# A graph layer's weighted one-hots: two wide VectorE operations per six chunks, or six tensor_scalar operations with place and weight as scalars

## The chip, the cores and the metric

The kernel runs on one core of a Trainium2 chip. The metric is the time on the device in microseconds (us), the median of three runs. A profile of one further execution was taken; all durations below come from it.

## The reference, cut to what matters

```python
# first layer: a weighted sum over edges (200,000 edges sorted by dst, 12,500 nodes of 256 numbers)
msgs = layernorm(x)[src] * edge_weight[:, None]
agg  = segment_sum(msgs, dst)            # indices sorted
x    = x + agg @ W.T + b
# second layer: a graph attention over 131,072 other edges gives each node four gates;
# four experts (256 -> 512 -> 256, gelu) run on every node
y    = layernorm(x)
x    = x + sum_e gate[:, e] * (gelu(y @ W1[e] + b1[e]) @ W2[e] + b2[e])
```

Everything is float32. The change concerns the first layer's `agg`.

## The kernel before, in words

The kernel has four stages, one after another. First, the inputs are normalised and written to DRAM as rows (`z_rows`), and the edge lists are turned into tiles. Second comes the gather stage, which is where the change lies. Third, `agg` goes through W, is normalised again and is stored. Fourth, the four experts run, beside the attention's gathers and scans, and after them the gates and the output.

In the gather stage the 200,000 edges are cut into chunks of 128 edges, one edge in each partition. Six chunks (`GQ = 6`) are a group, and there are 261 groups (`NQ`). The destinations are sorted, so all edges of a group usually lie within a window of 128 nodes that begins at the group's first destination. The function `window` (L485) makes the window's sum:

- For each chunk, GpSimd (POOL) issues one indirect DMA that fetches the 128 source rows of `z_rows` into a third of a tile `gt` (L497). The pool of `gt` has six such tiles, two to a group, so POOL can be up to three groups ahead of the readers.
- VectorE (DVE) makes six weighted one-hot matrices of 128 x 128, as one tile `oh_w`. The entry in row p and column l is the edge's weight where the destination's place in the window (mod 128, `lo_q`) is l, and else zero. The pool of `oh_w` has two such tiles.
- TensorE (PE) multiplies the six one-hots with the six row blocks and sums them in a PSUM tile `win` (L509). A float32 product is two matmul records and two weight loads.
- `add_window` (L511) adds `win` to the accumulator `acc_x` in two operations, one for each of the two node tiles that a window can touch (L515).

Before the change the one-hots take two VectorE operations. `spread_hot` (L312) compares a table of column numbers, each number twice, with the six places: a tensor_tensor in bfloat16 into `hit_w` (L316). A second tensor_tensor multiplies it with the weights into `oh_w`, float32, and reorders it on the way (L503):

```python
hit = spread_hot(hot, lo[:, s], P, "hit_w", GQ, 1)
oh = hot.tile([P, GQ, P], F32, name="oh_w")
nc.vector.tensor_mul(oh.rearrange("p (k i) l -> p k i l", i=2), hit.rearrange("p k l i -> p k i l"), ...)
```

Beside the groups runs a counting sort of the second layer's edges. In the first 32 groups (`early`) PE counts places (`count`, L330). At group 32 `sort_begin` (L359) turns the counts into starting places through small tables (`cn`, `inc`, `node`, `has`, `last`, `begin`). In the other 229 groups the generator `sort_all` emits its 1035 steps evenly, 4.5 to a group. A step is a chain on PE and ScalarE (ACT): a look-up (`look`, L411 and L413), an addition of one-hots (`place`, L416), a copy by ACT (`next`, L419) and a move (`perm`, L450) whose moving operand `st` DVE makes with one tensor_scalar (L444). For each eight steps DVE also makes the one-hots `oh_hi`, `oh_lo` and `to_p` (L316), two selections `sel` (L424) and `pos` (L426), and four small operations on eight numbers (L435 to L438).

Each engine runs its own list in order. The lists are made by a planner that goes by its own estimates of duration; a change in an operation can therefore change the order in which the planner puts others beside it. An instruction that waits holds up all that are behind it on its engine.

A further branch, which repeats `window` for groups that reach beyond one window, is guarded by a value computed at run time; in the profile L497 ran for 1563 chunks and L503 for 261 groups, which is once per group.

Of the kernel before, what the change touches and what calls it, by code (L numbers as in the profile page):

```python
# [23 lines left out]
F32 = mybir.dt.float32  # L24
# [3 lines left out]
BF = mybir.dt.bfloat16  # L28
AF = mybir.ActivationFunctionType
ALU = mybir.AluOpType  # L30
# [4 lines left out]
P = 128  # L35
N, D = 12500, 256
NT = 98
# [3 lines left out]
GQ = 6  # L41
NQ = (E + GQ * P - 1) // (GQ * P)
TB = 8
# [17 lines left out]
def gnn_gat_moe(ctx, tc, x, src, dst, edge_weight, W, b, W_gat, att_src, att_dst, b_gat, ln_gamma,  # L61
                ln_beta, W1, b1, W2, b2, edge_index, out):
    nc = tc.nc
# [65 lines left out]
    free = first_two.tile([P, P], F32, name="free")  # L129
# [33 lines left out]
    with ExitStack() as s1:  # L163
        edges = s1.enter_context(tc.tile_pool(name="edges", bufs=1))
# [58 lines left out]
        for g in range(NG):  # L223
            t0, n, _ = rows_of(g)
# [21 lines left out]
        as_int = prep.tile([P, NQ * GQ], I32, name="chunk_rows_f")  # L246
        nc.vector.tensor_copy(as_int, dst_f)
        nc.vector.tensor_scalar(as_int, as_int, P - 1, None, ALU.bitwise_and)
        lo_q = edges.tile([P, NQ * GQ], BF, name="lo_q")
        nc.vector.tensor_copy(lo_q, as_int)  # L250
        beyond = prep.tile([P, NQ * GQ], F32, name="chunk_rows_f")
        nc.vector.tensor_scalar(beyond, ahead.rearrange("p q j -> p (q j)"), float(P), float(P),
# [18 lines left out]
        for k in range(0, NQ, P):  # L271
            n = min(P, NQ - k)
# [36 lines left out]
        hot = s1.enter_context(tc.tile_pool(name="hot", bufs=2))  # L309
        gat = s1.enter_context(tc.tile_pool(name="gathered", bufs=6))  # L310

        def spread_hot(pool, v, width, name, n=TB, bufs=2):  # L312

            t = pool.tile([P, n // 2, width, 2], BF, name=name, bufs=bufs)
            shape = [P, n // 2, width, 2]
            nc.vector.tensor_tensor(  # L316
                t, twice[:, None, :width, :].to_broadcast(shape),
                v.rearrange("p (k i) -> p k i", i=2)[:, :, None, :].to_broadcast(shape),
                ALU.is_equal)
            return t  # L320
# [8 lines left out]
        count2 = acc.tile([NT, P], F32, name="place")  # L329
# [4 lines left out]
                nc.tensor.matmul(into, one(oh, i), one(ol, i), start=(c0 + i == 0),  # L334
                                 stop=(c0 + i == total - 1))

        def prefix(counts, name):

            cn = edges.tile([NT, P], F32, name="cn_" + name)
            nc.vector.tensor_copy(cn, counts)  # L340
            rs = small.tile([NT, 1], F32, name="row_sum")
            nc.vector.tensor_reduce(rs, cn, AX.X, ALU.add)
            pp = bank()
            nc.tensor.matmul(pp[:NT, 0, 0:1], after[:NT, :NT], rs, start=True, stop=True)
            first = small.tile([NT, 1], F32, name="first")
            nc.vector.tensor_copy(first, pp[:NT, 0, 0:1])
            inc = edges.tile([NT, P], F32, name="inc_" + name)
            nc.vector.tensor_tensor_scan(inc, ones[:NT, :], cn, first, ALU.mult, ALU.add)
            return cn, inc

# [6 lines left out]
        state = {}  # L357

        def sort_begin():  # L359
            cn, inc = prefix(count2, "2")  # L360
            node = edges.tile([NT, P], F32, name="node")
            nc.gpsimd.iota(node, pattern=[[1, P]], base=E2, channel_multiplier=P,
                           allow_small_or_imprecise_dtypes=True)
            has = edges.tile([NT, P], F32, name="has")
            nc.vector.tensor_scalar(has, cn, 0.0, None, ALU.is_gt)
            by_node(has, has2)
            last = edges.tile([NT, P], F32, name="last")
            nc.vector.tensor_scalar(last, inc, -1.0, 0.0, ALU.add, ALU.max)
            by_node(last, end2)
            begin = edges.tile([NT, P], F32, name="begin")  # L370
            nc.vector.tensor_sub(begin, inc, cn)
            nc.vector.tensor_sub(last, begin, node)
            nc.vector.tensor_mul(last, last, has)
            nc.vector.tensor_add(last, last, node)
            by_node(last, seg2)

            place = state["place"] = acc.tile([NT, P], F32, name="place")
            nc.tensor.matmul(place, ident[:NT, :NT], begin, start=True, stop=False,
                             skip_group_check=True)
            state["next"] = begin  # L380
# [109 lines left out]
        def window(q, idx, lo, w, chunks):  # L490

            n = len(chunks)
            rows = [gat.tile([P, GQ // 2, D], F32, name="gt") for _ in range(2)]
            rows = [rows[j * 2 // GQ][:, j % (GQ // 2), :] for j in range(n)]
            for j in range(n):
                c = chunks[0] + j
                nc.gpsimd.indirect_dma_start(out=rows[j], out_offset=None, in_=Z,  # L497
                                             in_offset=IND(ap=idx[:, c:c + 1], axis=0))

            s = slice(chunks[0], chunks[0] + GQ)  # L500
            hit = spread_hot(hot, lo[:, s], P, "hit_w", GQ, 1)
            oh = hot.tile([P, GQ, P], F32, name="oh_w")
            nc.vector.tensor_mul(oh.rearrange("p (k i) l -> p k i l", i=2),  # L503
                                 hit.rearrange("p k l i -> p k i l"),
                                 w[:, s].rearrange("p (k i) -> p k i", i=2)[:, :, :, None]
                                 .to_broadcast([P, GQ // 2, 2, P]))
            win = ps.tile([P, D], F32, name="win")
            for j in range(n):
                nc.tensor.matmul(win, oh[:, j, :], rows[j], start=(j == 0), stop=(j == n - 1))  # L509
            return win  # L510

        def add_window(at, win, m0, m1):
# [6 lines left out]
        for q in range(NQ):  # L519
            if q % 4 == 0:  # L520
                n = min(4, NQ - q)
# [4 lines left out]
            win = window(q, src1, lo_q, w1,  # L526
                         [c for c in range(c0, c0 + GQ) if c * P < E])
# [19 lines left out]
        with tc.If(further > 0):  # L547
            shift = edges.tile([P, 1], F32, name="shift")
            idx4 = edges.tile([P, GQ], I32, name="idx4")
            lo4 = edges.tile([P, GQ], F32, name="lo4")  # L550
            lob4 = edges.tile([P, GQ], BF, name="lob4")
            node4 = edges.tile([P, GQ], I32, name="node4")
            w4 = edges.tile([P, GQ], F32, name="w4")
            ahead4 = edges.tile([P, GQ], F32, name="ahead4")
            below4 = edges.tile([P, GQ], F32, name="below4")
            m01 = edges.tile([P, 2], F32, name="m01")
            with tc.For_i(0, NQ, 1) as q:
                nc.vector.memset(shift, 0.0)
                n = nc.values_load(more[0:1, bass.ds(q, 1)], min_val=0, max_val=NT,
                                   skip_runtime_bounds_check_because=BOUND)  # L560
                with tc.For_i(0, n, 1) as j:
                    nc.vector.tensor_scalar_add(shift, shift, float(P))
                    nc.vector.tensor_copy(idx4, src1[:, bass.ds(q * GQ, GQ)])
                    nc.vector.tensor_copy(w4, w1[:, bass.ds(q * GQ, GQ)])
                    nc.vector.tensor_copy(ahead4, further_by.rearrange("p q j -> p (q j)")[
                        :, bass.ds(q * GQ, GQ)])
                    nc.vector.tensor_copy(m01[:, 0:1], first_f[:, bass.ds(q, 1)])
                    nc.vector.tensor_scalar(lo4, ahead4, m01[:, 0:1], None, ALU.add)
                    nc.vector.tensor_copy(node4, lo4)
                    nc.vector.tensor_scalar(node4, node4, P - 1, None, ALU.bitwise_and)  # L570
                    nc.vector.tensor_copy(lob4, node4)
# [6 lines left out]
                    win = window(q, idx4, lob4, w4, range(GQ))  # L578
# [110 lines left out]
    with ExitStack() as s3:  # L689
# [71 lines left out]
        t = pre.tile([P, L2], F32, name="scan")  # L761
# [49 lines left out]
        with ExitStack() as s5:  # L811
# [22 lines left out]
            for g in range(NG):  # L834
                t0, n, _ = rows_of(g)
# [3 lines left out]
                for e in range(C):  # L839
# [60 lines left out]
        v = by_head(end, f[:, 1, :])  # L900
# [160 lines left out]
```

## Time and profile before

| what | value |
|---|---|
| median of three runs | 5190.45 us (5141.08, 5190.45, 5194.08) |
| the profiled execution's own time | 4425.88 us |
| its span, first to last instruction | 4424.1 us |
| granted TensorE clock, mean over the span | 0.909 |
| gather stage, first gather to last window added | 154.8 to 2290.6 us |
| POOL gathers L497 | 1563, mean 1059 ns |
| VectorE L316 into `hit_w` | 261, median 550 ns |
| VectorE L503 into `oh_w` | 261, mean 948 ns |
| TensorE L509 | 3126 records, mean 402 ns |

The profile gives the busy time of each engine, the idle time ahead of each group of instructions with what ended it, and the instructions in order of time. The median of the runs is 764.6 us above the profiled execution. The views describe the profiled execution only.

### The profile page before, as it was taken

The page shows a single profiled execution, that of the slowest core. Times are in us where ns is not written, and L with a number is a line of the kernel's source. Part 1 is how long each engine was busy: PE and PEld are TensorE (multiplying, and loading weights), DVE is VectorE, ACT ScalarE, POOL GpSimd, SP SyncE. Part 2 cuts the span into 40 slices and gives each one's busy share as a digit, 9 for nine tenths or more (in the row PEclk, how much of TensorE's full clock was granted, in tenths as well). Part 3 has the DMA queues.
Part 4 walks back from the last instruction along what each step waited for, and adds up shares of the span by engine and source line. Part 5 has one row for each costly group of instructions (what it writes and reads, how often), then busy time and mean ns, then how long its engine had stood idle before and what let it go on. Part 6 is the DMA issues. An engine that isn't in the chain of part 4 may idle for free. (4 is left out here: it accounts for less than half of the span.)

```text
span 4424.1 us, 54111 instructions
## 1 busy us (share of the span) xinstructions
PE 3583.0 (81%) x19146; PEld 2567.4 (58%) x19347; DVE 2584.5 (58%) x6116; ACT 1000.2 (23%) x2139; POOL 2956.1 (67%) x2822
## 2 busy tenths in 40 slices
PE   1377999999999999999988849899999989999000
PEld 0265766766676666667667736566656656566000
DVE  5577888888888888888875441221221221221368
ACT  5100322322222222222322112121221221222000
POOL 0477777777777777777765467777777777770720
PEclk6788999999999999999998769999999999999555
DMA  6433333333333333333335552222222222221759
GB/s 216 131 92 94 97 97 97 100 97 98 98 98 98 97 98 97 99 98 98 97 106 152 136 130 56 60 65 56 69 66 56 67 54 65 65 62 44 224 121 375
DMA packets 330548, 456.42 MB, mean 103 GB/s; under 512 B 82471, under 2 KB 258753, under 8 KB 328993
## 3 DMA queue, kind: packets, MB, share of 16 engines
q0 software_dynamic: 114128, 217.01, 20.1%
q1 hardware_dynamic: 163279, 204.96, 13.9%
q10 hardware_dynamic: 52866, 30.96, 2.3%
q8 instruction: 152, 2.49, 0.2%
q14 instruction: 123, 1.01, 0.1%
HBM read 332.00 MB, written 120.72 MB: 102 GB/s over the span
## 5 line engine op out<-in xcount | busy, mean ns | idle before, releaser
L497 POOL DMA_INDIRECT gt<-z_rows,src x1563 | 1655.4, 1059 | 628.1 <-issue 351.4
L712 POOL DMA_INDIRECT G<-gat_nodes,order x1024 | 1033.0, 1009 | 341.3 <-issue 291.7
L509 PE MATMUL win<-gt,oh_w 128*128 128x256 f32 x3126 | 854.2, 402 | 208.8 <-DMA gt<-z_rows,src 117.1
L509 PEld LDWEIGHTS win<-gt,oh_w 128*128 128x128 f32 x3126 | 560.9, 195 | 380.9 <-DMA gt<-z_rows,src 219.5
L852 PE MATMUL po<-w,hh 128*128 128x256 f32 x3136 | 708.6, 384 | 71.5 <-DVE fo L854 63.2
L854 DVE TENSOR_TENSOR fo<-po,b 128x256 f32<-128x256 f32 x392 | 165.6, 424 | 1018.5 <-PE po L852 1003.0
L852 PEld LDWEIGHTS po<-w,hh 128*128 128x128 f32 x3136 | 603.1, 193 | 200.2 <-DVE fo L854 66.0
L844 PE MATMUL ph<-yt,w 128*128 128x512 f32 (+1 forms) x1600 | 696.0, 588 | 3.1 <-DMA w<-in_L_ffn_W 3.1
L419 ACT ACTIVATE next<-place 98x128 f32<-98x128 f32 x1023 | 282.4, 276 | 1396.3 <-PE place L416 1395.1
L444 DVE TENSOR_SCALAR st<-along,place_l,code 128x1024 bf16<-128x1024 f16 x1024 | 548.8, 566 | 33.8 <-PE perm L450 23.2
L450 PE MATMUL perm<-st,to_p 128*128 128x512 bf16 x1848 | 549.3, 381 | 4.5 <-DVE st L444 2.8
L844 PEld LDWEIGHTS ph<-yt,w 128*128 128x128 f32 x1600 | 307.2, 192 | 335.3 <-issue 322.7
L846 ACT ACTIVATE hh<-ph,b 128x512 f32<-128x512 f32 (+1 forms) x400 | 270.3, 678 | 988.0 <-PE ph L844 979.9
L413 PE MATMUL look<-next,oht 98*128 98x128 f32 x2046 | 471.1, 312 | 0.8 <-ACT next L419 0.7
L413 PEld LDWEIGHTS look<-next,oht 98*128 98x128 f32 x2046 | 309.6, 190 | 172.7 <-ACT next L419 129.9
L515 DVE SCALAR_TENSOR_TENSOR acc_x<-win,in,acc_x 128x256 f32 x522 | 249.7, 478 | 253.2 <-PE win L509 252.4
L503 DVE TENSOR_TENSOR oh_w<-hit_w,w 128x768 f32<-128x768 bf16 x261 | 247.6, 948 | 0.5
L416 PE MATMUL place<-oh_lo,oh_hi 128*98 128x128 bf16 x1023 | 229.1, 224 | 0.4 <-ACT next L419 0.4
L411 PE MATMUL look<-oh_lo,same_hi 128*128 128x128 bf16 x1024 | 220.3, 220 | 5.7
L450 PEld LDWEIGHTS <-to_p 128*128 128x128 bf16 x2048 | 173.3, 98 | 55.8 <-issue 5.8
L424 DVE TENSOR_TENSOR sel<-look,oh_lo 128x512 f32<-128x512 f32 x256 | 175.3, 685 | 25.0 <-PE look L413 23.7
L402 ACT ACTIVATE same_hi<-bank 128x512 bf16<-128x512 f32 x256 | 152.9, 597 | 141.7 <-PE bank L401 135.6
(274 smaller groups left out, 3628.9 us busy)
## 6 DMA issues: line engine op xcount, KB each, us to landing
expert_rows<-fo SPq DMA_DIRECT2D x96, 512.0 KB, 2.8
fo_in<-expert_rows SPq DMA_DIRECT2D x24, 2048.0 KB, 14.9
gt<-z_rows,src POOLq DMA_INDIRECT x1563
xt<-in_x SPq DMA_DIRECT2D x48, 512.0 KB, 5.1
G<-gat_nodes,order POOLq DMA_INDIRECT x1024
z_rows<-xt ACTq DMA_DIRECT2D x24, 512.0 KB, 3.0
x_rows<-x SPq DMA_DIRECT2D x24, 512.0 KB, 5.6
y_t<-yt SPq DMA_DIRECT2D x48, 256.0 KB, 6.0
```

The lines of the kernel that those rows point to most:

```text
L413: nc.tensor.matmul(look[:, i % GT, :], b["oht"][:, i, :], state["next"], start=False, stop=True)
L419: nc.scalar.activation(nxt, place, AF.Copy)
L444: nc.vector.tensor_scalar(st, along, b["l"][:, i:i + 1], code2[:, c:c + 1], ALU.is_equal, ALU.mult)
L450: nc.tensor.matmul(perm[:, h, :], to_p, st[:, h * 512:(h + 1) * 512], start=(c == 0), stop=(c == NC2 - 1), skip_group_check=True)
L497: nc.gpsimd.indirect_dma_start(out=rows[j], out_offset=None, in_=Z, in_offset=IND(ap=idx[:, c:c + 1], axis=0))
L503: nc.vector.tensor_mul(oh.rearrange("p (k i) l -> p k i l", i=2), hit.rearrange("p k l i -> p k i l"), w[:, s].rearrange("p (k i) -> p k i ...
L509: nc.tensor.matmul(win, oh[:, j, :], rows[j], start=(j == 0), stop=(j == n - 1))
L515: nc.vector.scalar_tensor_tensor(to, win, m, to, ALU.mult, ALU.add)
L712: i = nc.gpsimd.indirect_dma_start(out=G[:, t + 1, :HC + H], out_offset=None, in_=NODE, in_offset=IND(ap=order[:, t:t + 1], axis=0))
L844: nc.tensor.matmul(ph[:, :n * P], w_1[:, e, k, f * P:(f + 1) * P], yt[:, k, :n * P], start=(k == 0), stop=(k == 1))
L846: nc.scalar.activation(hh[:, f, :n * P], ph[:, :n * P], AF.Gelu, bias=b_1[:, e * NF + f:e * NF + f + 1])
L852: nc.tensor.matmul(po, hh[:, f, i * P:(i + 1) * P], w_2[:, e, f, :], start=(f == 0), stop=(f == NF - 1))
```

## The change

Each chunk's one-hot becomes one tensor_scalar: the float32 row of column numbers (`free`) is compared with the chunk's place as one per-partition scalar and multiplied by the chunk's weight as a second one. Six of these write the six parts of `oh_w`. The tile `hit_w` is gone, and the places `lo_q` are kept in float32 rather than bfloat16. The first matmul of a group gets an explicit dependency on the last of the six operations. The small tables of `sort_begin` no longer have tiles of their own: they lie in one tile taken from the pool of `gt`, so that the iota that fills `node` moves on POOL from the start of the kernel to between two gathers of group 32. In the guarded branch the bfloat16 copy `lob4` of the places goes away likewise.

```diff
-        lo_q = edges.tile([P, NQ * GQ], BF, name="lo_q")
+        lo_q = edges.tile([P, NQ * GQ], F32, name="lo_q")
...
-        def prefix(counts, name):
-            cn = edges.tile([NT, P], F32, name="cn_" + name)
+        def prefix(counts, table):
+            cn = table[:, 0, :]
...
-            inc = edges.tile([NT, P], F32, name="inc_" + name)
+            inc = table[:, 1, :]
...
         def sort_begin():
-            cn, inc = prefix(count2, "2")
-            node = edges.tile([NT, P], F32, name="node")
+            table = gat.tile([P, GQ // 2, D], F32, name="gt").rearrange("p a (b e) -> p (a b) e", e=P)
+            table = table[:NT]
+            cn, inc = prefix(count2, table)
+            node, has, last = (table[:, k, :] for k in (2, 3, 4))
...
-            s = slice(chunks[0], chunks[0] + GQ)
-            hit = spread_hot(hot, lo[:, s], P, "hit_w", GQ, 1)
             oh = hot.tile([P, GQ, P], F32, name="oh_w")
-            nc.vector.tensor_mul(oh.rearrange("p (k i) l -> p k i l", i=2),
-                                 hit.rearrange("p k l i -> p k i l"),
-                                 w[:, s].rearrange("p (k i) -> p k i", i=2)[:, :, :, None]
-                                 .to_broadcast([P, GQ // 2, 2, P]))
+            for j in range(n):
+                c = chunks[0] + j
+                last = nc.vector.tensor_scalar(oh[:, j, :], free, lo[:, c:c + 1], w[:, c:c + 1],
+                                               ALU.is_equal, ALU.mult)
             win = ps.tile([P, D], F32, name="win")
             for j in range(n):
-                nc.tensor.matmul(win, oh[:, j, :], rows[j], start=(j == 0), stop=(j == n - 1))
+                i = nc.tensor.matmul(win, oh[:, j, :], rows[j], start=(j == 0), stop=(j == n - 1))
+                if j == 0:
+                    tc.add_manual_dep(i.ins, last.ins.name, mybir.DependencyInfo(
+                        mybir.DependencyClass.Sync, mybir.DependencyReason.DATA),
+                        reason="all the one-hots of the group")
             return win
```

More of the change, by code (lines that the diff above doesn't have):

```diff
@@ L310, in gnn_gat_moe, with spread_hot @@
         gat = s1.enter_context(tc.tile_pool(name="gathered", bufs=6))
-        def spread_hot(pool, v, width, name, n=TB, bufs=2):
-            t = pool.tile([P, n // 2, width, 2], BF, name=name, bufs=bufs)
-            shape = [P, n // 2, width, 2]
+        def spread_hot(pool, v, width, name):
+            t = pool.tile([P, TB // 2, width, 2], BF, name=name)
+            shape = [P, TB // 2, width, 2]
             nc.vector.tensor_tensor(
@@ L359, in sort_begin @@
         def sort_begin():
-            cn, inc = prefix(count2, "2")
-            node = edges.tile([NT, P], F32, name="node")
+            table = gat.tile([P, GQ // 2, D], F32, name="gt").rearrange("p a (b e) -> p (a b) e", e=P)
+            table = table[:NT]
+            cn, inc = prefix(count2, table)
+            node, has, last = (table[:, k, :] for k in (2, 3, 4))
             nc.gpsimd.iota(node, pattern=[[1, P]], base=E2, channel_multiplier=P,
                            allow_small_or_imprecise_dtypes=True)
-            has = edges.tile([NT, P], F32, name="has")
             nc.vector.tensor_scalar(has, cn, 0.0, None, ALU.is_gt)
             by_node(has, has2)
-            last = edges.tile([NT, P], F32, name="last")
             nc.vector.tensor_scalar(last, inc, -1.0, 0.0, ALU.add, ALU.max)
@@ L550, in gnn_gat_moe @@
             lo4 = edges.tile([P, GQ], F32, name="lo4")
-            lob4 = edges.tile([P, GQ], BF, name="lob4")
             node4 = edges.tile([P, GQ], I32, name="node4")
@@ L570, in gnn_gat_moe @@
                     nc.vector.tensor_scalar(node4, node4, P - 1, None, ALU.bitwise_and)
-                    nc.vector.tensor_copy(lob4, node4)
+                    nc.vector.tensor_copy(lo4, node4)
                     nc.vector.tensor_scalar(ahead4, ahead4, shift, None, ALU.subtract)
@@ L577, in gnn_gat_moe @@
                     nc.vector.tensor_copy(m01[:, 1:2], in1[:, bass.ds(q, 1)])
-                    win = window(q, idx4, lob4, w4, range(GQ))
+                    win = window(q, idx4, lo4, w4, range(GQ))
                     a = nc.values_load(tile0[0:1, bass.ds(q, 1)], engines=(mybir.EngineType.DVE,),
```

## The prediction

> **What bounds the kernel now.** I read the page's groups of instructions first, then the stretches of the gather stage, then GpSimd's waits in it, then the instructions in order of time. Three engines look full in the gather stage, so busy shares don't decide it:
>
> ```profile
> L497 POOL DMA_INDIRECT gt<-z_rows,src x1563 | 1655.4, 1059 | 628.1 <-issue 351.4
> L509 PE MATMUL win<-gt,oh_w 128*128 128x256 f32 x3126 | 854.2, 402 | 208.8 <-DMA gt<-z_rows,src 117.1
> L503 DVE TENSOR_TENSOR oh_w<-hit_w,w 128x768 f32<-128x768 bf16 x261 | 247.6, 948 | 0.5
> ```
>
> In a steady stretch (columns: stretch, length, then PE, weight loads, DVE, ACT, POOL):
>
> ```profile
> 1000.00:1500.00 500.00, 472.31 (x3183) 345.66 (x3239) 432.81 (x908) 146.60 (x382) 387.53 (x370) 1.00 0.34 98
> ```
>
> 370 gathers are 61.7 groups, so a group takes 8.11 us. PE has 0.45 us of it idle, DVE 1.09, POOL 1.82. But PE's idle time ends with a gather's landing (L509 above), and POOL's waits in the sort part of the stage, last column the longest, say what its idle time is:
>
> ```profile
> POOL gt L497 <- issue: 301.1, 988, 0.3
> POOL gt L497 <- PE win L509: 29.6, 97, 0.3
> ```
>
> No wait exceeds 0.3 us, whatever is named: it is a fixed gap of 0.305 us behind every gather, not a wait for a buffer. 1562 gaps are 476 us, and with 152 us before the first gather that is all of the 628 idle. So POOL issues without a stop from 154.8 us to 2286.3: 1563 x (1.059 + 0.305) = 2132 us, the whole stage. PE works off a group 2.5 to 4.2 us after its last gather, and a window is added about 13 us before its buffer is wanted again: the others follow POOL.
>
> What can POOL save? The tile's own view has least, median and longest:
>
> ```profile
> L497 POOL DMA_INDIRECT gt<-z_rows,src x1563: 942/949/2273, 154.8 to 2285.3; - x196
> ```
>
> A gather takes 0.945 us unless something stretches it; 1563 x (1.059 - 0.945) = 178 us are stretch. The timeline shows by what:
>
> ```profile
> 1201.78 0.94 DVE L503 TENSOR_TENSOR oh_w<-hit_w,w 128x768 f32<-128x768 bf16 x1
> 1201.91 1.62 POOL L497 DMA_INDIRECT gt<-z_rows,src  x1 [0.30 <-PE bank L401]
> ...
> 1203.84 0.95 POOL L497 DMA_INDIRECT gt<-z_rows,src  x1 [0.30 <-issue]
> ...
> 1204.72 0.95 DVE L503 TENSOR_TENSOR oh_w<-hit_w,w 128x768 f32<-128x768 bf16 x1
> ...
> 1205.10 1.39 POOL L497 DMA_INDIRECT gt<-z_rows,src  x1 [0.31 <-issue]
> ...
> 1216.36 1.71 DVE L444 TENSOR_SCALAR st<-along,place_l,code 128x1024 bf16<-128x1024 f16 x3
> ...
> 1217.16 1.04 POOL L497 DMA_INDIRECT gt<-z_rows,src  x1 [0.30 <-issue]
> ```
>
> The gather at 1201.91 is 0.68 too long: what ran 0.12 us after its start, `oh_w`, ended 0.81 after it. At 1205.10 it is 0.44, with the end at 0.57. So a gather reads something 0.12 us in and waits until the wide operation ends. The gather among three `st`, 1.71 us without a break, loses only 0.09.
>
> [...] `st`, if it starts 0.16 us or more before the gather's read, delays it, and if later is itself delayed, so that the lock begins some 0.27 us into its 0.54. [...]
>
> **The change part by part.**
>
> *Removed: stretch.* I assigned every stretched gather to the two-input tensor_tensor running 0.12 us after its start. `oh_w`: 158 gathers, 67 us; `hit_w`: 51 gathers, 16 us, together 83. Check: an operation holding a lock for L delays a gather by L*L/(2 x 1.364) on average. The lock seems to begin 0.15 us in, so L is 0.80 and 0.40 us: 0.235 + 0.059 us per group, 77 us for 261. Value -83, ends -70 and -95. `oh_hi`, `oh_lo`, `to_p` (48 us) and `st` with the unassigned (43) stay; more gathers meet them per us, but there is less time: nothing.
>
> *Added: the locks of 1563 tensor_scalars of 128x128.* The nearest row is L105, float32, two per-partition scalars, 256 columns:
>
> ```profile
> 2340.60 1.36 DVE L105 TENSOR_SCALAR y<-x,mv,rstd 128x256 f32<-128x256 f32 x4
> ```
>
> One takes 0.406 us (its median); start to start it is (1.36 - 0.406)/3 = 0.318. [...] A gain is excluded, since nothing of it frees POOL; that six in a row act as one lock is excluded by the three `st` above. Value +3, ends 0 and +66.
>
> *DVE's own time.* Removed: 0.87 + 0.47 us start to start (426.97 to 427.84; 444.18 to 444.65) = 1.34 per group. Added: 6 x 0.25 = 1.50, plus the wait when GpSimd holds the lock, some 0.24 us late in each gather: 0.24/1.33 of the operations by 0.12 on average, 0.02 each, 0.13 in all. The built order puts about three of each eight steps' one-hots between the four small dependent operations, whose gaps of some 0.13 they fill: -0.1. Net +0.2 of 1.09 idle. POOL takes 0.3 away; 0.6 is left, so this costs nothing; without that cover it would be 0.2 x 261 = 52 us.
>
> *PE's wait.* The first matmul of a group waited for the single `oh_w`; it waits for the last of six now, and the other five for their gathers only. Queued behind it are the look-up chain and through it `next` on ACT and `st` on DVE. The `oh_w` ended a median 11.8 us, at least 3.4, before its group's first addition. In the new order part of a group's six stands behind the previous group's additions, which wait for PE. That eats from the lead, and POOL has 13 us before it notices. Value 0. PE's order changes otherwise only in where the same matmuls stand.
>
> *Moved: the iota and the tables.* The iota took 0.23 us at 2.5; with a gap it costs POOL 0.5 at group 32. The table's slot is wanted again 15 gathers later, about 20 us; the tables' last reader came 9 us after the first writer. POOL may lose 0 to 5: value +1. `lo_q` in float32 lies ahead of the stage, beside DMA: 0. Lists of SP are unchanged; the guarded branch didn't run.
>
> *Sum* against the profiled execution: -83 + 3 + 1 = -79 us, 4425.9 to 4347. The following stages start when the gathers end and keep their lengths.
>
> **How that stands to the median.** The runs are 764.6 us above the profiled execution; no view says where. If gathers still bound the stage there, the saving is the same and the median becomes 5190 - 79 = 5111. I don't scale it.
>
> **The rivals.**
> - *In the timed runs another engine bounds the gather stage.* PE idles only 0.45 us per group; were part of the 765 us PE at a lower clock, POOL would wait and its stretch be hidden. For: the gap itself, and the expert stage is full of PE. Against: the spare 13 us and the clock of 1.00 in the profile. What stays is the first 32 groups, 0.32 x 32 = 10 us: 5180.
> - *The lock lasts the whole instruction.* [...] Against: the timing of `st`. -83 + 66 = -17: 5173.
> - *Slower: DVE becomes the bound,* because GpSimd's hold delays each one-hot in full. For: 0.24 us late in each gather, and DVE is 87% busy. Against: `st` has a mean of 566 ns and a median of 541, only 25 ns of delay. DVE decides above 8.11 - (7.02 - 1.34) = 2.43 us per group for six, 0.405 each. At 0.25 + 0.24 = 0.49 the group takes 8.62: +0.51 x 261 = 133 us, 5323.
>
> That the change does nothing can't be: the operations are in the built lists, six for two.
>
> **Numbers.** About 1%, 52 us, is what a measurement here can tell from no change. Chances: forecast 0.55 (own range 5085 to 5145), other engine 0.25, whole-instruction lock 0.08, slower 0.12. Nearly nine tenths of the forecast lie below 5138, 0.48, with 0.04 from the two no-change cases: faster 0.52; slower 0.11, nearly all of the last rival; the rest 0.37. The range reaches from 5060 (both removed locks at their upper end, and the runs' own scatter of 53 us) to 5220 (the no-change cases with scatter); left out are the slower rival and small tails.
>
> **What would show it.** Right: L497's mean falls from 1059 to about 1008 ns, no stretched gather has an `oh_w` beside it, POOL's gaps stay at 0.3 us and the last gather starts near 2207 instead of 2285. The new operation shows 0.34 us. Wrong: POOL's waits for PE longer than 0.3 us (an engine behind it decides), one-hots well above 0.4 us (DVE), or L497's mean near 1050 (longer locks). If the profiled time falls by 79 and the median doesn't, the first rival holds.

## The result, and the profile after

The changed kernel took 5330.22 us (median of 4 runs, 5317.92 to 5342.21), beside 5192.26 us for the kernel before (4 runs). The ratio is 1.026, 95% interval 1.021 to 1.031: slower by 138 us, where 5111 was forecast and the range ended at 5220.

The runs of this study met chips of two kinds. On two chips the kernel before took a median of 5196 and 5295 us, on four others 4421 to 4429 us, with a scatter within each set of some 2% on the first two and 0.5% on the others. By their times, the three runs shown before the prediction are of the first kind, and the profiled execution of before (4425.88 us) is of the second. Below they are called the first kind and the second kind of chip. One of the four was met twice and was of the same kind both times; the others were met once, so it is not shown further that a chip keeps its kind. Every ratio of an experiment is between runs on one chip; for the ratio above the chip is not on record. Ratios leave out executions over 1.5% above the fastest of their kernel, which medians keep, so the two can differ by some tenths of a per cent.

The profile after was taken on the first kind (its own time 5317.92 us, span 5316.2 us, granted TensorE clock 0.863). Its groups of instructions, in the columns busy, mean and idle time:

```profile
L497 POOL DMA_INDIRECT gt<-z_rows,src x1563 | 1626.2, 1040 | 1281.2 <-PE win L506 593.2 <-issue 390.9 <-DMA z_rows<-xt 155.2
L506 PE MATMUL win<-gt,oh_w 128*128 128x256 f32 x3126 | 822.8, 410 | 115.4 <-DVE oh_lo L316 88.8 <-DMA gt<-z_rows,src 25.4 <-DVE oh_w L502 0.5
L502 DVE TENSOR_SCALAR oh_w<-free,lo_q,w 128x128 f32<-128x128 f32 x1563 | 474.0, 351 | 3.4 <-DMA z_rows<-xt 3.4
L413 PE MATMUL look<-next,oht 98*128 98x128 f32 x2046 | 523.4, 341 | 460.0 <-ACT next L419 301.4 <-issue 140.2 <-ACT oht L391 10.6
```

The same stretch of 500 us as before (PE, weight loads, DVE, ACT, POOL), GpSimd's waits from 600 to 2290 us (in total, times, longest), and the gather's tile:

```profile
1000.00:1500.00 500.00, 401.83 (x2492) 294.86 (x2493) 340.09 (x883) 115.63 (x296) 283.03 (x283) 0.89 0.26 75
```

```profile
POOL gt L497 <- PE win L506: 401.6, 67, 11.6
POOL gt L497 <- issue: 237.4, 776, 0.7
```

```profile
L497 POOL DMA_INDIRECT gt<-z_rows,src x1563: 941/949/3021, 157.8 to 2909.2; - x196
```

GpSimd does not issue without a stop here: in that stretch it waits 67 times for TensorE's windows, up to 11.6 us at a time, and its last gather starts at 2909 us instead of 2285. In 500 us there are 283 gathers where there were 370. The new operation costs what was forecast: 0.35 us in the mean (0.34 its median). And TensorE hardly stands at the first matmul of a group: of its 115.4 us of idle time there, 88.8 lie ahead of the stage, and 0.5 are for a one-hot. It stands at the look-ups, for ScalarE's `next`.

So two questions follow: why does the kernel before take 5190 us where its profile says 4426, and where do 138 us come from if not from a wait for one-hots?

### The profile page after: what moved, and what is told of

It reads as the page before. It is cut to its first block, busy times and chain, and to the rows that moved or that the text cites. A ratio compares the mean times of both kernels' runs of the same rounds, so it can differ in the third digit from the quotient of the medians.

```text
span 5316.2 us, 55422 instructions
## 1 busy us (share of the span) xinstructions
PE 3845.8 (72%) x19346; PEld 2741.6 (52%) x19347; DVE 2629.9 (49%) x7157; ACT 1007.4 (19%) x2139; POOL 2911.3 (55%) x2822
## 5 line engine op out<-in xcount | busy, mean ns | idle before, releaser
L497 POOL DMA_INDIRECT gt<-z_rows,src x1563 | 1626.2, 1040 | 1281.2 <-PE win L506 593.2
L506 PE MATMUL win<-gt,oh_w 128*128 128x256 f32 x3126 | 822.8, 410 | 115.4 <-DVE oh_lo L316 88.8
L853 PE MATMUL po<-w,hh 128*128 128x256 f32 x3136 | 767.0, 402 | 174.1 <-ACT hh L847 115.4
L413 PE MATMUL look<-next,oht 98*128 98x128 f32 x2046 | 523.4, 341 | 460.0 <-ACT next L419 301.4
L853 PEld LDWEIGHTS po<-w,hh 128*128 128x128 f32 x3136 | 627.3, 202 | 342.5 <-ACT hh L847 136.9
L845 PE MATMUL ph<-yt,w 128*128 128x512 f32 (+1 forms) x1600 | 723.6, 603 | 77.5 <-ACT hh L847 68.9
L506 PEld LDWEIGHTS win<-gt,oh_w 128*128 128x128 f32 x3126 | 620.8, 206 | 230.2 <-issue 93.0
L413 PEld LDWEIGHTS look<-next,oht 98*128 98x128 f32 x2046 | 346.5, 210 | 687.9 <-ACT next L419 449.3
L450 PE MATMUL perm<-st,to_p 128*128 128x512 bf16 x2048 | 666.7, 413 | 4.9 <-DVE st L444 3.9
L502 DVE TENSOR_SCALAR oh_w<-free,lo_q,w 128x128 f32<-128x128 f32 x1563 | 474.0, 351 | 3.4 <-DMA z_rows<-xt 3.4
```

The costliest lines, as they stand in the source:

```text
L413: nc.tensor.matmul(look[:, i % GT, :], b["oht"][:, i, :], state["next"], start=False, stop=True)
L450: nc.tensor.matmul(perm[:, h, :], to_p, st[:, h * 512:(h + 1) * 512], start=(c == 0), stop=(c == NC2 - 1), skip_group_check=True)
L502: last = nc.vector.tensor_scalar(oh[:, j, :], free, lo[:, c:c + 1], w[:, c:c + 1], ALU.is_equal, ALU.mult)
L506: i = nc.tensor.matmul(win, oh[:, j, :], rows[j], start=(j == 0), stop=(j == n - 1))
L845: nc.tensor.matmul(ph[:, :n * P], w_1[:, e, k, f * P:(f + 1) * P], yt[:, k, :n * P], start=(k == 0), stop=(k == 1))
```

## The experiments

Lengths of stages below are read from the instructions in order of time: the counting part runs from the first gather to the first addition of group 32, the sort part from there to the last addition of a window.

### The kernel before once more

No edit. (Chip of the first kind.)

> The kernel before, profiled again, since its timed runs (5192) lie 17% above its profiled execution (4426) and the changed kernel's profile (5316) doesn't. Theory A (TensorE bounds the gather stage in the timed runs, POOL doesn't): about 5192, and a profile that, where it lies near the median, shows POOL waiting for PE by several us and the stretch of the gathers hidden. Theory B (POOL bounds it in the timed runs too): POOL's gaps stay at 0.3 us.

Measured: 5187.86 us, 0.999 (0.996 to 1.001). This time the profile was of the same kind as the runs (the last line is the stretch of 500 us, with granted clock, DMA share and GB/s at its end):

```profile
L497 POOL DMA_INDIRECT gt<-z_rows,src x1563 | 1631.2, 1044 | 1148.6 <-PE win L509 508.1 <-issue 390.8 <-DVE hit_w L316 152.0
L509 PE MATMUL win<-gt,oh_w 128*128 128x256 f32 x3126 | 852.6, 416 | 95.0 <-DVE hit_w L316 86.7 <-DMA gt<-z_rows,src 4.2 <-DVE oh_w L503 2.6
L413 PE MATMUL look<-next,oht 98*128 98x128 f32 x2046 | 516.3, 337 | 357.8 <-ACT next L419 233.5 <-issue 114.6 <-ACT same_hi L402 6.6
1000.00:1500.00 500.00, 408.42 (x2524) 298.49 (x2522) 340.57 (x707) 116.38 (x297) 297.72 (x289) 0.89 0.27 76
```

GpSimd waits 508 us for windows here; on the second kind of chip every such wait was the fixed 0.3 us. The gather stage is TensorE's on this chip, together with the look-up chain that TensorE shares with ScalarE: TensorE is not full (408 of 500 us busy), but GpSimd waits for it. From the first gather until `order` is written it takes 2649 us, not 2145, and the experts' stage (first to last `fo`) 1703, not 1431: nearly all of the 765 us between the profile and the median lie in these two. What the change cost lies in the gather stage alone: 2773 us after, 2649 here, +123, of which the counting part has 35 (352 against 317) and the sort part 90 (2414 against 2324).

Could the changed kernel have met a slower chip of the first kind, such as the one at 5295? The experts' stage, which the change leaves as it was, says no: it took 1693 us in the changed kernel's profile, 1703 here, and 1734 in a profile on the chip at 5295.

### No one-hots, the tables alone, no dependency

Three kernels beside it, on the same chip. The first reuses the one-hots of the first two groups for all others; so it leaves out 1551 of the 1563 tensor_scalars, and the dependency with them (and cannot tell the two apart):

```diff
-            oh = hot.tile([P, GQ, P], F32, name="oh_w")
...
+            oh = fixed_oh[done[2] % 2]
+            done[2] += 1
+            if done[2] <= 2:
...
```

> The changed kernel with the one-hots of the first two groups used for all 261, so that VectorE makes 12 of 1563 (the sums are left wrong). Theory A1 (TensorE waits for late one-hots behind VectorE's list): back to 5192 or below. Theory A2 (TensorE is slower by itself in the changed kernel's order of matmuls, whatever VectorE does): stays at about 5330.

Measured: 5217.03 us, 1.006 (1.003 to 1.009). Its gathers are no longer stretched by one-hots (a mean of 1002 ns, where the kernel before has 1044), and the time gains nothing:

```profile
L498 POOL DMA_INDIRECT gt<-z_rows,src x1563 | 1565.5, 1002 | 1195.3 <-PE win L509 487.5 <-issue 389.2 <-DVE oh_w L505 155.8
```

The gathers are 66 us shorter in all, and GpSimd's idle time ahead of them is 47 us longer (1195 against 1149). Of that idle time a little less than before is laid to windows (488 against 508), and more to other instructions of TensorE's. That most of GpSimd's saving goes into waiting is the mechanism of the prediction's first rival, seen directly.

The second has the tables and the iota of the change with the one-hots of before:

```diff
-            cn = edges.tile([NT, P], F32, name="cn_" + name)
+            cn = table[:, 0, :]
...
```

> The changed kernel with the two wide operations of before for the one-hots and bfloat16 places: of the change only the tables in a gt tile and the moved iota are left. If the one-hots cost the time: about 5192. If the tables do: about 5330.

Measured: 5193.69 us, 0.998 (0.995 to 1.001). The tables cost nothing that can be measured.

The third is the changed kernel without the explicit dependency:

```diff
-                if j == 0:
-                    tc.add_manual_dep(i.ins, last.ins.name, ...)
```

> The changed kernel without the explicit dependency, each matmul waiting for its own one-hot. If the wait for the last of six costs the time: below 5330, towards 5192. If six waits cost more than one: above 5330. If neither: 5330.

Measured: 5178.37 us, 0.997 (0.993 to 1.000). Without the dependency nothing is lost: it costs the difference to 1.026, some 150 us, and the gather stage of the two profiles differs by as much (2773 us with it, 2623 without). TensorE's idle time ahead of the look-ups:

```profile
L413 PE MATMUL look<-next,oht 98*128 98x128 f32 x2046 | 509.8, 333 | 375.2 <-ACT next L419 203.2 <-issue 168.1 <-ACT oht L391 1.2
```

It is 375 us, against 460 with the dependency and 358 in the kernel before.

There are two ways in which a dependency can cost this. TensorE waits for the last one-hot (theory W). Or the planner, which now sees the first matmul of a group ready later, writes other lists (theory O). What a place in a list can cost is seen in the profile after: VectorE stood 2.84 us ahead of a `sel` (646.60 us) until TensorE's look-up was done, and the one-hot behind it, for which the profile names no wait, started at 647.21. The built lists do differ. In the sort part TensorE's list has 112 blocks of six window matmuls in a row before the change, 125 without the dependency and 181 with it. Between an addition (`place`) and the next look-up, which needs ScalarE's copy, there is neither a window matmul nor a batch of transposes or `same_hi` in 425, 424 and 468 places (the 437 in two expectations below is a miscount of the 424). VectorE's list of the counting part differs too. In both, the last one-hot of a group stands behind the additions of the group before (30 of 31 groups); with the dependency the group's first one-hots stand ahead of these additions in 29 groups, without it in one.

### The order imposed

To tell W from O, TensorE's matmuls of the sort part were put in a given order, each tied to the one ahead of it by an edge that orders and doesn't wait:

```diff
+        for k in ORDER:
+            ins = on[k][at_pe[k]]
+            at_pe[k] += 1
+            if before_it is not None:
+                tc.add_manual_dep(ins, before_it.name, mybir.DependencyInfo(
+                    mybir.DependencyClass.NoSync, mybir.DependencyReason.DATA), ...)
+            before_it = ins
```

`ORDER` holds one letter per matmul. In order: the kernel before in the changed kernel's order; the changed kernel in the order without the dependency; the new one-hots without the dependency, with window matmuls dealt out in pairs; the same with all in blocks of six.

> The kernel before with its own one-hots and no explicit dependency; only TensorE's matmuls of the sort part stand in the order that they have in the changed kernel (each is tied to the one ahead of it by an edge that orders and doesn't wait). Theory O, the order: the dependency makes the planner put window matmuls in blocks of six, so that fewer of them are left to stand between an addition (place) and the next look-up, where TensorE waits for ScalarE's copy (next). Then this kernel loses what the changed one loses in the sort part, 90 us: 5188 + 90 = about 5280. Theory W, the wait: TensorE loses the time standing at the first matmul of a group. There is no such wait here: 5190, no change.

> The changed kernel with its dependency on the last one-hot; only the matmuls of the sort part stand in the order that they have without the dependency. Theory O: the sort part's 90 us come back, the counting part, whose order is not touched, keeps its loss of some 25: 5330 - 90 = about 5240, and not above 5260. Theory W: the wait is still there, 5330.

> The new one-hots without the dependency. The other matmuls of the sort part stand as they do there, but the window matmuls are dealt out two at a time behind the additions that have no other matmul of a batch (transposes, same_hi) between them and the next look-up: such gaps fall from 437 to 1. Theory O: TensorE's idle time ahead of the look-ups on next (about 358 us in the profile without the dependency, 0.82 us per such gap) is filled. As far as it was truly idle that comes off 5178; if half of it was, about 5000, and at least below 5130. Theory W: nothing changes, 5178.

> The new one-hots without the dependency. The six window matmuls of every group stand together at the place of the last one, 225 blocks of six instead of 125; the other matmuls stand as they do there. Gaps with nothing but moves and look-ups between an addition and the next look-up rise from 437 to about 508. Theory O: 71 gaps at 0.82 us, 58 us: about 5236. Theory W: there is no wait for the last one-hot, 5178.

Measured, on a chip of the second kind (4421.94 us for the kernel before): 0.998 (0.997 to 0.999), 0.996 (0.995 to 0.998), 1.005 (1.003 to 1.007), 1.001 (1.000 to 1.002). Where GpSimd bounds the stage neither theory can show: TensorE's idle time ahead of the look-ups on `next` was 1.0, 0.7, 0.2 and 21.9 us there. The differences of some tenths of a per cent go with the gathers' stretch (means of 1049, 1045, 1073 and 1055 ns, 1059 in the kernel before) in the first three. In the last, with all windows in blocks, the gathers are shorter and the kernel still isn't faster; there GpSimd's waits for windows reach 2.7 us even on this kind of chip:

```profile
POOL gt L511 <- PE win L520: 41.9, 112, 2.7
```

That is in the direction of theory O, but small. The gain that was expected of the pairs on the first kind of chip did not show here, where there was no such idle time to fill, and is untried there.

The first two were run again, with the changed kernel itself and one that has the dependency in the last 229 groups alone (`if j == 0 and (not isinstance(q, int) or q >= early)`):

> The changed kernel as it is. On a chip where the kernel before takes some 5190 us: 1.026 of it again. On one where it takes 4422 and GpSimd bounds the gathers: the kernel with the same one-hots and the dependency, but the other order of matmuls, was at 0.996; the sort part's order cost nothing there (the kernel before in the changed order was at 0.998), so 0.996 to 1.000.

> The kernel before, only with TensorE's matmuls of the sort part in the changed kernel's order; the same kernel as the one run before under that description, which met a chip at 4422 us. On a chip at 5190, theory O (the order costs the time): 1.017. Theory W (the wait for the last one-hot, or the later one-hots, costs it): 1.000. On a chip at 4422: 0.998 again.

> The changed kernel with the dependency, only with TensorE's matmuls of the sort part in the order that they have without it; also met a chip at 4422 us before. On a chip at 5190, theory O: 1.008, the counting part's loss alone. Theory W: 1.026, as the changed kernel. On a chip at 4422: 0.996 again.

> The changed kernel without the dependency in the first 32 groups (counting part), with it in the 229 others, where TensorE's order is the changed kernel's. The counting part took 352 us with the dependency and 327 without on the chip at 5190; VectorE's list has the last one-hot behind the window before only with it. So 25 us less than the changed kernel there, 1.021 of the kernel before. On a chip at 4422 the counting part with the dependency took 329 us and 284 in the kernel before, so some 40 us less than the changed kernel: 0.987 to 0.991.

Measured, on another chip of the second kind (4421.44 us before): 0.997 (0.996 to 0.998), 0.997 (0.995 to 0.998), 0.995 (0.994 to 0.997), 0.996 (0.995 to 0.997). So the same change that costs 2.6% on the first kind of chip gains 0.3% on the second, 11 us of medians. The last of the four missed its expectation: without the dependency the counting part is 315 us instead of 324, not 40 less. Its premise was wrong as well: the last one-hot stands behind the window before with and without the dependency.

### Where the forecast gain went on the second kind of chip

The changed kernel's profile on it (4410.61 us, span 4408.9 us) is the one to hold against the prediction's profile:

```profile
L497 POOL DMA_INDIRECT gt<-z_rows,src x1563 | 1634.4, 1046 | 630.0 <-issue 347.3 <-DMA z_rows<-xt 154.3 <-PE win L506 37.5
```

The gathers are back to back again, but their mean is 1046 ns, not 1008. Working out the stretch as the prediction did, gather by gather, gives 139 us before and 84 after in the stretch from 480 to 2300 us (1333 and 1363 gathers): `oh_w` and `hit_w` with 73 us are gone, `oh_lo` and `to_p` rose from 12 to 35. In the counting part it went the other way. The gathers up to 440 us, before and then after (least, median, longest):

```profile
L497 POOL DMA_INDIRECT gt<-z_rows,src x201: 942/1042/1648, 156.3 to 439.9; - x101
```

```profile
L497 POOL DMA_INDIRECT gt<-z_rows,src x175: 942/946/2972, 156.8 to 439.1; - x175
```

Fewer gathers are stretched, but some by 2 us. The timeline of the changed kernel shows how:

```profile
295.80 0.68 DVE L316 TENSOR_TENSOR oh_lo<-twice,lo 128x1024 bf16<-128x1024 bf16 x1
295.83 2.55 POOL L497 DMA_INDIRECT gt<-z_rows,src  x1 [0.30 <-issue]
...
296.40 0.56 DVE L316 TENSOR_TENSOR oh_hi<-twice,hi 128x784 bf16<-128x784 bf16 x1
...
296.88 0.68 DVE L316 TENSOR_TENSOR oh_lo<-twice,lo 128x1024 bf16<-128x1024 bf16 x1
297.48 0.59 DVE L502 TENSOR_SCALAR oh_w<-free,lo_q,w 128x128 f32<-128x128 f32 x2
```

and that of the kernel before a like run of wide comparisons:

```profile
303.69 0.68 DVE L316 TENSOR_TENSOR oh_lo<-twice,lo 128x1024 bf16<-128x1024 bf16 x1
303.92 1.28 POOL L497 DMA_INDIRECT gt<-z_rows,src  x1 [0.30 <-issue]
304.29 0.56 DVE L316 TENSOR_TENSOR oh_hi<-twice,hi 128x784 bf16<-128x784 bf16 x1
...
304.76 0.68 DVE L316 TENSOR_TENSOR oh_lo<-twice,lo 128x1024 bf16<-128x1024 bf16 x1
```

An unstretched gather ends 0.82 us after its read at 0.12. The one at 303.92 ends at 305.20, which is 0.83 after the end of the one `oh_lo` that it met (304.37). The one at 295.83 ends at 298.38, 0.82 after the end of the third wide comparison (297.56): it let two more pass. The counting part took 324 us instead of 284, +40, the sort part 1790 instead of 1852, -62.

Is this due to how the new one-hots stand among the wide comparisons? A kernel with the old pair in the counting part and the new one-hots, without the dependency, after it:

```diff
+            if isinstance(q, int) and q < early:
+                hit = spread_hot(hot, lo_first[:, s], P, "hit_w", GQ, 1)
+                nc.vector.tensor_mul(oh..., hit..., w[:, s]...)
+            else:
+                for j in range(n):
+                    nc.vector.tensor_scalar(oh[:, j, :], free, lo..., w..., ALU.is_equal, ALU.mult)
```

> The two wide operations of before in the first 32 groups (counting part), the new tensor_scalars without the dependency in the other 229. On a chip where the kernel before takes 4422: the counting part lost 40 us with the changed one-hots (gathers held over two or three of its wide comparisons in a row), the sort part gained 55; if the loss is due to how the one-hots stand in the counting part, it goes and 0.986 to 0.989 is left; if it is due to anything else in the change (the tables, the float32 places), the 0.997 stays. On a chip at 5190: the kernel without the dependency took 0.997 and its counting part 10 us more than before's: 0.994 to 0.996.

Measured, second kind (4426.6 us before): 4377.99 us, 0.989 (0.988 to 0.991). The counting part is back at 283 us, and the sort part keeps most of its gain (1803 us). Its gathers:

```profile
L499 POOL DMA_INDIRECT gt<-z_rows,src x1563 | 1605.4, 1027 | 630.4 <-issue 339.1 <-DVE hit_w L318 154.7 <-PE place L418 35.6
```

The mean is 1027 ns. That the changed one-hots in the counting part cost the 40 us is shown: in the profiles of this kind of chip that part takes 283 to 284 us in all seven with the old pair there, and 315 to 329 us in all seven with the new operations, with the dependency or without. Why a gather lets three comparisons pass there and only one in the kernel before is not shown.

### The wait without the order, on the first kind of chip

Beside it the two imposed orders were run once more, on the second kind again:

> The kernel before with TensorE's matmuls of the sort part in the changed kernel's order, the same kernel as twice before, for a chip at 5190. Theory O (the order costs the time): 1.017. Theory W (the wait for the last one-hot, or one-hots that come later): 1.000. On a chip at 4422: 0.997 again.

> The changed kernel with its dependency, TensorE's matmuls of the sort part in the order that they have without it, the same kernel as twice before, for a chip at 5190. Theory O: 1.008, the counting part's loss alone. Theory W: 1.026, as the changed kernel. On a chip at 4422: 0.996 again.

Measured: 0.996 (0.994 to 0.997) and 0.995 (0.993 to 0.997).

Then a kernel with the old pair in the counting part, the new one-hots with the dependency in the other 229 groups, and TensorE's order as it is without the dependency (`if j == 0 and isinstance(q, int) and q >= early`, and `ORDER` as above):

> The two wide operations of before in the counting part, so that it is as before; in the other 229 groups the new tensor_scalars with the dependency on the last of the six, and TensorE's matmuls of the sort part in the order that they have without the dependency. On a chip at 5190, theory O (the order that the dependency brings costs the time): no loss, 0.993 to 0.997. Theory W (the wait for the last one-hot costs it): the sort part's share of the loss stays, 1.014 to 1.020. On a chip at 4422: 0.986 to 0.989, as the kernel with the pair in the counting part and no dependency.

Measured, on a chip of the first kind (5294.54 us before): 5249.9 us, 0.994 (0.991 to 0.997). Its groups:

```profile
L513 POOL DMA_INDIRECT gt<-z_rows,src x1563 | 1568.6, 1004 | 1230.8 <-PE win L530 553.2 <-issue 383.5 <-DVE hit_w L326 155.0
L530 PE MATMUL win<-gt,oh_w 128*128 128x256 f32 x3126 | 854.3, 419 | 138.2 <-DVE hit_w L326 88.8 <-DVE oh_w L526 39.0 <-issue 6.3
L428 PE MATMUL look<-next,oht 98*128 98x128 f32 x2046 | 498.5, 327 | 358.9 <-ACT next L434 259.1 <-issue 87.8 <-ACT same_hi L417 5.0
```

TensorE does wait for the last one-hot here, 39.0 us against 0.5 in the changed kernel, and still nothing is lost. In the sort part the wait is not what costs, and what the dependency costs there comes with the lists that the planner makes of it. Two limits remain: the changed kernel itself was not run on this chip, and the planner's lists for the other engines were not held fixed.

The two last runs were to show whether TensorE's changed order costs the time by itself, first in the kernel before, then with the old pair in the counting part and the new one-hots without the dependency after it. Both met the second kind of chip:

> The kernel before with its own one-hots and without any dependency, TensorE's matmuls of the sort part in the changed kernel's order. On a chip at 5190 (or 5290), where the changed one-hots with the dependency and the order without it were at 0.994: if the changed order alone costs the time, 1.015 to 1.020; if it needs the later one-hots as well, 1.000. On a chip at 4422: 0.996 again.

> The two wide operations of before in the counting part, the new tensor_scalars in the other 229 groups, no dependency on the last one-hot; TensorE's matmuls of the sort part in the changed kernel's order. On a chip at 5190 to 5290: if the changed order costs the time by itself, 1.012 to 1.018; if it needs the dependency as well, 0.994, as the kernel with the dependency and the other order. On a chip at 4422, where the changed order alone was worth 3 to 5 thousandths and the pair in the counting part was at 0.989: 0.985.

Measured: 0.995 (0.993 to 0.996) against 4428.62 us, and 4363.34 us, 0.987 (0.985 to 0.989), against 4423.17. On the second kind of chip the last is the fastest of all, and the two gains nearly add up (in the profiles the gather stage is shorter by 50 us with the pair in the counting part, by 19 with the order alone, by 63 with both); on the first kind it is untried, and there its order is the suspect. The kernel with the pair, the dependency and the other order beats the kernel before on the first kind by 0.6%. It was not run on the second, where the changed kernel in the same order was at 0.995 to 0.996.

## Why the prediction was wrong

**The bound.** The forecast that GpSimd bounds the gather stage is right for the profile that it was read from, and wrong for the runs that were to be forecast. The step that failed first is "How that stands to the median": "If gathers still bound the stage there, the saving is the same". They don't: GpSimd waited 508 us for windows in the kernel before. The first rival had the mechanism. Its number, 5180, is met by the change without its dependency (5178) only by luck: its gain was to come from the first 32 groups, which went from 317 to 327 us, and what was gained came in the sort part (2324 to 2290). The spare 13 us and the clock of 1.00, which the prediction held against it, were the profile's own and no evidence on the runs. On the first kind of chip the granted clock from 1000 to 1500 us is 0.89, and nothing is spare: the median group's window ends when its buffer is wanted (0.0 us ahead, groups 40 to 249), where it was 13.7 us ahead on the second kind.

**"PE's wait ... Value 0."** The wait for the last one-hot costs nothing that was found, as forecast, though by luck: the argument rested on the slack behind a GpSimd that bounds. What failed is the sentence after it: "PE's order changes otherwise only in where the same matmuls stand", priced at nothing. On a chip where TensorE bounds, the dependency costs about 150 us (1.026 with it, 0.997 without), and in the sort part not by the wait (0.994 with the wait and the other order); in the counting part, where 25 us of it lie (352 against 327), the two were not told apart. No rival had it: the slower one was VectorE as the bound, whose mechanism is refuted by the new operation's 0.35 us and VectorE's 340 busy us in 500; that its 5323 lies near the 5330 measured is luck. By which piece of the lists the 150 us arise is open. TensorE's order of the sort part is the likeliest for its 90, from the idle time ahead of the look-ups (460 us against 358 and 375) and because the loss was gone where this order was replaced. It is not shown; the runs that had the order alone were on the other kind of chip. The wait at those look-ups is also not the 0.82 us per bare gap that I put into two expectations. In the changed kernel from 600 to 2600 us it is 143 waits with a longest of 7.2:

```profile
PE look L413 <- ACT next L419: 265.6, 143, 7.2
```

**Removed stretch, -83.** On the second kind of chip, where it can be held against a profile, the part by `oh_w` and `hit_w` went in the sort part as stated (73 us before, none after). What failed is that `oh_hi`, `oh_lo` and `to_p` (48 us) "stay", priced at "nothing". They rose by some 19 us in the sort part, and in the counting part some gathers waited for three comparisons in a row. The counting part lost 40 us, the sort part gained 62; the changed kernel's profile was 15 us below that of before, not 79.

**Added locks, +3; DVE's own time.** Right in size. What the prediction calls a lock is a hold that the profile before shows in both directions. Of the 147 gathers whose read, which the prediction puts 0.12 us after their start, fell 0.15 us or more into an `oh_w`, 143 ended 0.82 to 0.85 us after that `oh_w`. And all 129 `st` that began 0.38 to 0.52 us before a gather's end took 0.62 to 0.76 us, where the median `st` took 0.54. How long a new one-hot takes and holds, that profile did not show: the +3, its upper end of 66, and the 0.34 us for one operation and 0.25 from start to start that the sums use were my estimate. In the profile after it took 0.34 us (its median), 0.07 less than the 0.406 of 256 columns before, and 0.26 from start to start. By the prediction's own assignment, 71 gathers of the second kind's profile whose read met one ended 0.03 to 0.15 us late, 4.5 us in all. VectorE was never the bound: from 1000 to 1500 us it was busy for 340 us in the profile after, and for 456 in the changed kernel's profile on the second kind. The reading of `st` was too early: in the profile before, of 43 gathers whose read fell 0.16 to 0.22 us into an `st` only 4 waited to its end or longer, and of those at 0.26 us or more all did. None of the sums used the 0.16.

**Moved iota and tables, +1.** Right: 0.998.

**The chances.** The case that the runs were in, another engine as the bound, was given a quarter. A profile 17% away from the median, with no view that explains it, deserved more than half for "the runs have another bound", and then every view of that profile is a statement on another case.

## What to carry to other kernels

When the profiled execution and the timed runs differ by more than their scatter, find out first whether they have the same bound; until then a saving on the profile's critical engine is worth nothing certain. An explicit dependency is also an input to the planner: compare the built lists with and without it, or keep the order by edges that don't wait, since the lists can cost more than the wait (here the sort part took 90 us more, and a wait of 39.0 us cost nothing that was found). And where VectorE's wide two-input operations hold up GpSimd's gathers, as `oh_w` and `hit_w` did here for 73 us of the sort part, removing some of them changes how the others meet the gathers (`oh_lo` and `to_p` rose from 12 to 35 us), so the count has to be made again on the new order.

## What the runs showed of the hardware

- Chips of one type differed by up to a fifth on one kernel: 4421 to 4429 us on four chips, 5196 and 5295 on two. The difference lies where TensorE is nearly full on the faster kind (busy for 472 us of 500 from 1000 to 1500 us, and for 947 of 1000 from 3000 to 4000): the gather stage took 2145 and 2649 us, the experts 1431 and 1703. The granted clock (means over a run of 0.84 to 0.89 on the first kind, 0.90 to 0.93 on the second) explains only part. From 1000 to 1500 us it was 1.00 and 0.89, and a group took 8.1 and 10.4 us (370 and 289 gathers). TensorE's busy time in a group rose from 7.7 to 8.5 us, about as the clock fell; its idle time rose from 0.45 to 1.9. Much of that idle time shows at the look-ups, as waits for ScalarE's `next` (234 us in all, under 1 on the second kind), and `next` itself waits for TensorE's `place` (669 us of ScalarE's idle time ahead of it). Why the ring is slower beyond the clock is not shown.
- A gather whose read fell 0.15 us or more into an `oh_w` was held to its end (143 of 147 in the profile before): the one at 1201.91 in the profile before took 1.62 us instead of 0.95 and ended 0.81 us after the `oh_w` that it met. A gather could lose to the next ones too: the one at 295.83 in the changed kernel's profile on the second kind took 2.55 us, over three wide comparisons in a row. Having waited longest did not earn that gather the next turn.
- A tensor_scalar of 128x128 float32 with two per-partition scalars took 0.34 us (its median), and 1563 of them held gathers up by 4.5 us in all in a profile of the second kind, where the two-input operations that they replaced had held them up by 83.
